# A graph kernel's pattern stage: three settle groups, gathered candidate rows and split degree sums

## The chip, the cores and the metric

The kernel runs on one core of one Trainium2 chip. The metric is device time in microseconds (us); lower is better. PE is TensorE, DVE VectorE, ACT ScalarE, POOL GpSimd and SP SyncE, whose queue here only issues DMAs. PSUM is the memory that PE writes its results to. Line numbers (L823) are those of the kernel before, unless a text says otherwise.

## What is computed

Four graph layers work on 16 graphs (batches) of 1024 nodes with 128 features. Only the second layer matters here. It takes the 0/1 pattern of the adjacency matrix and thins it by a rule that runs over the rows in order, because each row's removals also clear a column:

```python
def step(carry, n):
    row = jnp.take(carry, n, axis=0)
    nbi = row.astype(jnp.int32)
    num = jnp.sum(nbi)
    sf = jnp.where(num > T_DIL, (num + K_DIL - 1) // K_DIL, 1)   # T_DIL = 10, K_DIL = 2
    rank = jnp.cumsum(nbi)
    rm = row & (rank % sf == 0)
    valid = (mask_b[n] != 0) & (num > 1)
    rm = jnp.where(valid, rm, False)
    keep = ~rm
    carry = carry.at[n].set(row & keep)
    carry = carry.at[:, n].set(carry[:, n] & keep)
```

A node with at most ten neighbours left drops all of them (sf is 1); a node with more drops those at rank h and 2h, with h about half the count. The thinned matrix is then used in three graph convolutions. The kernel uses the fact that very little of the matrix survives: for each graph it finds the at most 128 "candidates" that still have more than ten neighbours when their turn comes, settles what they remove by a few rounds of a fixed-point iteration, and treats all other nodes as empty, apart from "lone" ones that keep their own diagonal entry. Flags would send the program to a general path; with these inputs they do not.

## The kernel before, in words

The program has four stages, one after the other: attention (to about 1700 us of the profile), the pattern stage (1700 to about 2095 us), three convolutions, and the end with layers 3 and 4. The attention stage has written the 0/1 mask of every graph to DRAM as `mask_d`, in fp16. The change touches only the pattern stage, `phase_pattern` from L656 on.

Three kinds of task make up that stage; each is a Python generator, and each `yield` ends a step.

- `find(b)`, L751, once for each of 16 graphs, 11 steps. It loads the graph's mask `m` (2 MB, L754, on the SP queue; the pool has three buffers for it). Degrees are column sums: 64 matmuls with a column of ones (L760), copied by ACT (L764). POOL makes the strictly upper diagonal blocks `md` (L767, eight multiplies). Three passes of `earlier` (L777 and L781, 36 matmuls each) count the neighbours that come before a node and drop out; after the third, the candidates are known. `slots` (L711) numbers them and makes a one-hot `oh` (L719). L804 and `nodes` (L728) turn this into rows and columns of node numbers; `keep.node` (L729, ACT) and `keep.index` (L731, DVE) hold them for gathers. L810 gathers the candidates' 128 rows of the adjacency matrix from DRAM, 512 KB, by an indirect DMA on POOL's queue. Eight ACT instructions make `le` (L817). L823 takes the candidates' columns out of the mask: 64 matmuls of 128 columns, `m` against `oh`. DVE masks that into `base` (L831); L837 (eight matmuls) gives ranks. At the end the gathered rows are turned (L854), copied (L856) and multiplied (L860) into `V`.
- `settle(g)`, L864, for eight graphs side by side, so its wide DVE operations have 8 x 128 elements per partition. It has five rounds: nine small DVE operations, three wide ones (L896 to L898), eight one-column matmuls (L901), a copy back (L903). Then follow rank tests, a transpose and the store to `slots_d`.
- `alone(b)`, L956, four steps for each graph once its settle is done: rank matmuls (L964), ACT and DVE tests (L970, L972), a second `slots` and two gathers. `inner` (L735) turns node numbers into indices for the gathers of `x1` rows (L746).

`rolling` (L635) sets the order. It keeps one list of at most five open tasks, in the order of the list, and opens the next only when the last opened one has made two steps and all that it needs has ended; in each turn each open task makes one step. The list is ten finds, settle 0, finds and alones in turn, settle 1, the other alones. A settle at the head of the list that isn't ready holds up all behind it. The framework then places instructions in each engine's queue, near this order, and each engine works its own queue in order. After the tasks come the last gathers of lone rows.

Of the kernel before, what the change touches and what calls it, by code (L numbers as in the profile page):

```python
# [22 lines left out]
B, N, F = 16, 1024, 128  # L23
# [590 lines left out]

KEEP = 10
ROUNDS = 5
HALF = B // 2


# [12 lines left out]
    arrays["q_one_up"] = np.ascontiguousarray(np.broadcast_to(node[:P], (P, P)))  # L632


def rolling(tasks, depth, lag):  # L635


    todo, active, ended = list(tasks), [], set()
    while todo or active:
        while (  # L640
            todo and len(active) < depth and (not active or active[-1][2] >= lag)
            and all(n in ended for n in todo[0][2])
        ):
            active.append([todo[0][0], todo[0][1], 0])
            todo.pop(0)
        for a in list(active):
            try:
                next(a[1])
                a[2] += 1
            except StopIteration:  # L650
                active.remove(a)
                ended.add(a[0])
# [3 lines left out]
def phase_pattern(ctx, tc, t, c, mask_d, slots_d, x1_d, keep, flags):  # L656
# [78 lines left out]
    def inner(k0, k1):  # L735

        k = slice(k0, k1)
        at = sm.tile([P, HALF], F32, name="at")
        none = sm.tile([P, HALF], F32, name="none")
        nc.vector.tensor_scalar(at, keep.node[:, k], -1.0, 0.0, op0=ALU.add, op1=ALU.max)  # L740
        nc.vector.tensor_scalar(none, keep.node[:, k], 0.0, float(N), op0=ALU.is_equal, op1=ALU.mult)
        nc.vector.tensor_copy(keep.inner[:, k], at)
        nc.vector.tensor_tensor(keep.row[:, k], at, none, ALU.add)
# [7 lines left out]
    def find(b):  # L751
# [2 lines left out]
        nc.sync.dma_start(m, mask_d[b].rearrange("(t p) n -> p t n", p=P))  # L754
        yield

        pu = ps_s.tile([P, T], F32, name="pu", tag="ps")
        for ni in range(T):
            for ci in range(T):
                nc.tensor.matmul(  # L760
                    pu[:, ni : ni + 1], m[:, ci, ni * P : (ni + 1) * P], one, start=ci == 0, stop=ci == T - 1
                )
        deg = sm.tile([P, T], F32, name="deg", bufs=6)
        nc.scalar.copy(deg, pu)  # L764
        md = wp.tile([P, T, P], F16, name="md", bufs=3)
        for ti in range(T):
            nc.gpsimd.tensor_tensor(md[:, ti, :], m[:, ti, ti * P : (ti + 1) * P], less, ALU.mult)  # L767
# [44 lines left out]
            bass.IndirectOffsetOnAxis(ap=keep.index[:, b : b + 1], axis=0),  # L812
        )

        le = wp.tile([P, T, P], F16, name="le", bufs=3)
        for ti in range(T):
            nc.scalar.activation(le[:, ti, :], row, AF.Sign, bias=half_up[:, ti : ti + 1])  # L817
# [1 line left out]

        pg = ps_b.tile([P, T, P], F32, name="pg", tag="pb")  # L820
        for ni in range(T):
            for ci in range(T):
                nc.tensor.matmul(  # L823
                    pg[:, ni, :], m[:, ci, ni * P : (ni + 1) * P], oh[:, ci, :],
                    start=ci == 0, stop=ci == T - 1,
                )
# [36 lines left out]

    def settle(g):  # L864

        bs = slice(g * HALF, (g + 1) * HALF)
        shape = [P, HALF, P]

        def tiny(name):
            return sm.tile([P, HALF], F32, name=name, bufs=3)  # L870

        def wide(name, dtype=F16):
            return lp.tile(shape, dtype, name=name)
# [6 lines left out]
        rb = RB[:, bs, :]  # L880
        for k in range(ROUNDS):
            num, h, big, top = tiny("num"), tiny("h"), tiny("big"), tiny("top")
            nc.vector.scalar_tensor_tensor(num, num0[:, bs], 1.0, gone, op0=ALU.add, op1=ALU.subtract)

            nc.vector.tensor_scalar(h, num, 0.5, 0.25, op0=ALU.mult, op1=ALU.add)
            nc.vector.tensor_scalar(h, h, ROUND, None, op0=ALU.add)
            nc.vector.tensor_scalar(h, h, ROUND, None, op0=ALU.subtract)
            nc.vector.tensor_scalar(big, num, float(KEEP), None, op0=ALU.is_gt)


            nc.vector.scalar_tensor_tensor(v1[:, bs], h, EDGE - 1, gone, op0=ALU.add, op1=ALU.add)
            nc.vector.tensor_tensor(top, v1[:, bs], h, ALU.add)
# [5 lines left out]
            nc.vector.tensor_tensor(rm, e1, e2, ALU.max)  # L898
            pn = ps_s.tile([P, HALF], F32, name="pn", tag="ps")
            for j in range(HALF):  # L900
                nc.tensor.matmul(pn[:, j : j + 1], rm[:, j, :], one, start=True, stop=True)  # L901
# [5 lines left out]
        inner(g * HALF, (g + 1) * HALF)  # L907
# [8 lines left out]
        for j in range(HALF):  # L916
# [15 lines left out]
        nc.vector.scalar_tensor_tensor(k1, num, 1.0, k1, op0=ALU.is_le, op1=ALU.max)  # L932
# [3 lines left out]
        for j in range(HALF):  # L936
# [13 lines left out]
        for j in range(HALF):  # L950
# [5 lines left out]
    def alone(b):  # L956

        pb = ps_b.tile([P, N], F32, name="prank", tag="pb")
        for ti in range(T):
            lo = ti * P  # L960
            for at in (0, N // 2):
                n0, n1 = max(lo, at), at + N // 2
                if n0 < n1:
                    nc.tensor.matmul(  # L964
                        pb[:, n0:n1], base[:, b, ti, :], run[:, n0 - lo : n1 - lo],
                        start=ti == 0, stop=n0 == lo and n1 == lo + P,
                    )
# [26 lines left out]
        yield  # L994

    tasks = [(f"f{b}", find(b), []) for b in range(HALF + 2)]
    tasks.append(("s0", settle(0), [f"f{b}" for b in range(HALF)]))
    for b in range(HALF - 2):
        tasks += [(f"f{HALF + 2 + b}", find(HALF + 2 + b), []), (f"a{b}", alone(b), ["s0"])]
    tasks.append(("s1", settle(1), [f"f{b}" for b in range(HALF, B)]))  # L1000
    tasks += [(f"a{b}", alone(b), ["s0"]) for b in (HALF - 2, HALF - 1)]
    tasks += [(f"a{b}", alone(b), ["s1"]) for b in range(HALF, B)]
    rolling(tasks, 5, 2)
    inner(B, B + HALF)
    inner(B + HALF, 2 * B)
    for k in range(B, 2 * B):
        rows_of_x1(k)


    nc.vector.tensor_scalar(keep.lone, keep.lone, 1.0, None, op0=ALU.min)  # L1010

# [1202 lines left out]
```

## Time and profile before

| | us |
|---|---|
| median of 10 runs | 3215.98 |
| lowest and highest run | 3210.03, 3223.99 |
| the profiled execution, its time | 3215.18 |
| the profiled execution, its span | 3213.2 |
| first matmul of the pattern stage (L760) | 1700.8 from the span's start |
| last matmul of the pattern stage (L728) | 2094.1 |

The profile is of one execution, taken by the hardware. It lists for each engine how long it was busy and what ended its idle time. Over the whole span PE is busy for 88%, DVE 70%, ACT 55% and POOL 40%; a busy share of PE overstates its work, since matmuls overlap and each is drawn with its full length. A view of one stretch gives the same per engine, with the clock that TensorE was granted (PEclk, 1.00 is full) and the share of time in which the 16 DMA engines worked. Between 1700 and 2095 us PE is busy for 290.8 us, DVE 232.2, ACT 104.2 and POOL 122.6, the mean granted clock is 0.73 and the DMA share 0.32.

### The profile page before, as it was taken

Reading aid. Unit: us, or ns where it says so; the run is one execution under the profiler, and the core shown is the slowest. Engines: PE = TensorE matmul, PEld = TensorE weight load, DVE = VectorE, ACT = ScalarE, POOL = GpSimd, SP = SyncE. Lnnn points to the kernel's source line nnn. Section 1 sums busy time; section 2 is a strip of 40 time slices with the busy share of each in tenths; the row PEclk is TensorE's granted clock in tenths of the full one; section 3 lists DMA queues with packets and bytes.
Section 4 is the critical chain, followed back from the end, with each engine's and each line's share of the span. In section 5 each row is a group of like instructions: output and inputs, shape, how many; then the busy total and the mean of one; then the engine's idle time right before and its main releaser. Section 6 shows DMA issues by size and latency. Waiting matters only on the chain. (4 is left out here: it accounts for less than half of the span.)

```text
span 3213.2 us, 70693 instructions
## 1 busy us (share of the span) xinstructions
PE 2812.8 (88%) x25724; PEld 2495.9 (78%) x25724; DVE 2250.2 (70%) x8226; ACT 1781.8 (55%) x5608; POOL 1271.5 (40%) x1280
## 2 busy tenths in 40 slices
PE   5999999999999999999997959467787899999997
PEld 3877877778777877778786858366676899999997
DVE  5887878788787878788784565745555566666665
ACT  3877777677776777677772323145644234333342
POOL 5544555454545454453113423243323323332221
PEclk9999999999999999999996767788988899999999
DMA  6422333223322332222023522043443434444441
GB/s 178 117 70 76 83 98 83 61 78 98 98 59 77 94 98 76 67 78 72 21 99 124 180 96 91 17 153 139 152 171 146 159 134 163 173 160 166 156 147 30
DMA packets 162024, 348.62 MB, mean 108 GB/s; under 512 B 14709, under 2 KB 68231, under 8 KB 161537
## 3 DMA queue, kind: packets, MB, share of 16 engines
q1 hardware_dynamic: 149760, 311.37, 30.7%
q0 software_dynamic: 10752, 28.42, 3.0%
q10 hardware_dynamic: 1152, 4.19, 0.4%
q8 instruction: 206, 3.38, 0.4%
q14 instruction: 154, 1.25, 0.1%
HBM read 257.87 MB, written 87.03 MB: 107 GB/s over the span
## 5 line engine op out<-in xcount | busy, mean ns | idle before, releaser
L272 POOL TENSOR_SCALAR mask<-ld 104x1024 f16<-104x1024 f32 (+1 forms) x150 | 441.4, 2942 | 555.3 <-PE pw L354 233.4
L434 PE MATMUL pg<-parts,oh 104*128 104x384 f32 (+1 forms) x1760 | 539.8, 383 | 49.6 <-ACT hg L452 48.9
L465 PE MATMUL pa<-hg,we 128*104 128x129 f32 (+1 forms) x3520 | 568.2, 277 | 1.9
L446 DVE SCALAR_TENSOR_TENSOR junk<-pg,w_a 128x128 f32<-128x128 f32 x1600 | 405.8, 284 | 177.4 <-PE pg L439 174.6
L465 PEld LDWEIGHTS pa<-hg,we 128*104 128x104 f32 x3520 | 497.7, 175 | 32.2 <-ACT hg L452 18.9
L452 ACT ACTIVATE hg<-pg,hg 128x128 f32<-128x128 f32 x1600 | 511.2, 371 | 17.1
L439 PE MATMUL pg<-parts,oh 104*128 104x384 f32 (+1 forms) x1760 | 473.4, 343 | 0.0
L434 PEld LDWEIGHTS pg<-parts,oh 104*128 104x128 f32 x1760 | 282.8, 193 | 78.5 <-ACT hg L452 61.8
L439 PEld LDWEIGHTS pg<-parts,oh 104*128 104x128 f32 x1760 | 315.3, 193 | 0.0
L450 ACT ACTIVATE hg<-sc 128x2 f32<-128x2 f32 (+1 forms) x880 | 188.5, 216 | 168.1 <-DVE junk L446 163.3
L419 DVE TENSOR_TENSOR we<-k_id,ids 128x832 f32<-128x832 f16 (+1 forms) x240 | 228.3, 951 | 8.4 <-PE pa L465 5.1
L1343 POOL TENSOR_TENSOR rstd<-ve,mhalf 128x4 f32<-128x4 f32 x96 | 97.0, 1010 | 324.4 <-DVE ve L1342 324.2
L389 ACT CAST oh<-oh_b 104x1024 fp32r<-104x1024 bf16 (+1 forms) x240 | 221.3, 978 | 2.1 <-DVE oh_b L385 2.0
L291 PE MATMUL pw<-w_all,xT 128*104 128x512 f32 x320 | 187.5, 670 | 17.2 <-DMA xT<-in_xTp 8.3
L1347 DVE TENSOR_SCALAR x<-x,mv,rstd 128x128 f32<-128x128 f32 x256 | 102.8, 443 | 91.1 <-POOL rstd L1343 91.1
L357 ACT CAST qs<-pw 104x416 f16<-104x416 f32 (+1 forms) x240 | 114.6, 478 | 66.9 <-PE pw L354 63.2
L385 DVE TENSOR_TENSOR oh_b<-pw,k_slot_edge 104x512 bf16<-104x512 f32 (+1 forms) x240 | 144.7, 635 | 9.7 <-PE pw L384 7.2
L364 DVE SCALAR_TENSOR_TENSOR one_way<-qs,mask 104x1040 bf16<-104x1040 f16 (+9 forms) x160 | 148.8, 930 | 0.1
L1452 ACT ACTIVATE y<-x,shift,rstd 128x128 f32<-128x128 f32 x128 | 52.7, 482 | 162.9 <-POOL shift L1445 162.9
L500 POOL TENSOR_TENSOR own<-parts 104x128 f32<-104x128 f32 x160 | 96.9, 641 | 115.5 <-DVE x_rows L521 79.5
L378 ACT CAST oh_b<-pw 104x512 bf16<-104x512 f32 (+1 forms) x240 | 133.2, 556 | 14.5 <-PE pw L377 14.4
L336 DVE TENSOR_TENSOR g<-k_slot,off 105x1408 f16<-105x1408 f16 x80 | 132.6, 1657 | 11.6 <-ACT off L332 11.5
(356 smaller groups left out, 6688.7 us busy)
## 6 DMA issues: line engine op xcount, KB each, us to landing
ld<-in_adjT SPq DMA_DIRECT2D x135, 416.0 KB
m<-mask_d SPq DMA_DIRECT2D x16, 2048.0 KB
keep_adj<-in_adjT SPq DMA_DIRECT2D x8, 4096.0 KB
adj<-in_adjT SPq DMA_DIRECT2D x8, 4096.0 KB
mask_d<-mask SPq DMA_DIRECT2D x144, 208.0 KB
hT_d<-uT SPq DMA_DIRECT2D x48, 512.0 KB
h<-hT_d SPq DMA_DIRECT2D x48, 512.0 KB
hT<-hT_d SPq DMA_DIRECT2D x32, 512.0 KB
```

Of the source, the lines that this page charges most:

```text
L272: engine.tensor_scalar(mt[:n, s, :N], ld[:n], 0.0, None, op0=ALU.is_gt)
L291: nc.tensor.matmul(pw[:W], xT[:, s * W : (s + 1) * W], w_all, start=True, stop=False, skip_group_check=True)
L364: nc.vector.scalar_tensor_tensor(junk[:W, :nb, :], q[:W, at : at + nb, :W], EDGE, mt[:W, i, i * W : NP].rearrange("p (n w) -> p n w", w=W) ...
L385: nc.vector.tensor_tensor(o[:W, n0 : n0 + m, 1, :], pw[:W, :m, :], k_slot_edge[:W].unsqueeze(1).to_broadcast([W, m, C]), ALU.is_equal,)
L389: nc.scalar.copy(wide.ends[:W, n0 : n0 + m], o[:W, n0 : n0 + m])
L419: nc.vector.tensor_tensor(we[:, :n, :], k_id.unsqueeze(1).to_broadcast([P, n, W]), wide.ids[:, 2 * lo : 2 * hi].unsqueeze(2).to_broadcast( ...
L434: nc.tensor.matmul(flat[:, first : 3 * F], own, d.parts[i][:W, p, first:], start=p == 0, stop=False, skip_group_check=True,)
L439: nc.tensor.matmul(pg[:, 1::step, :], other, reversed_parts(d.parts[j][:W, p, :], step), start=False, stop=p == 1, skip_group_check=True,)
L446: nc.vector.scalar_tensor_tensor(junk, pg[:, 1 + e, :], 0.0, w_a2, op0=ALU.max, op1=ALU.mult, accum_out=d.sc[:, at + e : at + e + 1],)
L450: nc.scalar.activation(hg[:, u - lo, :ways, F], d.sc[:, at : at + ways], AF.Exp)
L452: nc.scalar.activation(hg[:, u - lo, e, :F], pg[:, 3 - 3 * e, :], AF.Copy, scale=hg[:, u - lo, e, F : F + 1])
L465: nc.tensor.matmul(PA[bank][:W, at : at + part.stop - part.start], we[:, 2 * (u - lo) + e, :], hg[:, u - lo, e, part], start=False, stop=T ...
```

## The change

It has four parts, all in the pattern stage.

1. Groups. Settle runs for groups of 6, 6 and 4 graphs instead of 8 and 8. `rolling` has a limit for each kind of task: four finds, one settle, two alones (with which the gathers of lone rows of `x1` now count, one task for each group). A task that isn't ready no longer holds up those of another kind.
2. Candidates' rows gathered and turned. The 64 matmuls of L823 go. In their place a second indirect DMA gathers the candidates' 128 rows of the mask from DRAM (256 KB, the mask is symmetric), and eight matmuls with a diagonal matrix (`there`, one more DVE operation) turn them. `m` is not read any more after the third pass.
3. Degrees. The first four of eight 128-node blocks are row sums by ACT (a Relu over 1024 elements with an accumulator); the other four stay column sums on PE, 32 matmuls.
4. Small operations. A settle round has seven small DVE operations instead of nine, by keeping a rounding constant inside `h`.

```diff
+GROUPS = ((0, 6), (6, 12), (12, 16))
...
-def rolling(tasks, depth, lag):
+def rolling(tasks, most, lag):
...
+        for task in list(todo):
+            name, kind, steps, after = task
+            same = [a for a in active if a[1] == kind]
+            if len(same) < most[kind] and (not same or same[-1][3] >= lag) and ended.issuperset(after):
+                active.append([name, kind, steps, 0])
+                todo.remove(task)
...
+        deg = sm.tile([P, T], F32, name="deg", bufs=6)
+        for ti in range(T // 2):
+            junk = wp.tile([P, N], F16, name="hit1")
+            nc.scalar.activation(junk, m[:, ti, :], AF.Relu, accum_out=deg[:, ti : ti + 1])
         pu = ps_s.tile([P, T], F32, name="pu", tag="ps")
-        for ni in range(T):
+        for ni in range(T // 2, T):
...
-        deg = sm.tile([P, T], F32, name="deg", bufs=6)
-        nc.scalar.copy(deg, pu)
+        nc.scalar.copy(deg[:, T // 2 :], pu[:, T // 2 :])
...
+        marks = wp.tile([P, N], F16, name="marks")
+        nc.gpsimd.indirect_dma_start(
+            marks, None, mask_d.rearrange("b n m -> (b n) m"),
+            bass.IndirectOffsetOnAxis(ap=keep.index[:, b : b + 1], axis=0),
+        )
+
+        there = sm.tile([P, P], F16, name="there")
+        nc.vector.tensor_scalar(there, same, keep.node[:, b : b + 1], 1.0, op0=ALU.mult, op1=ALU.min)
...
         for ni in range(T):
-            for ci in range(T):
-                nc.tensor.matmul(
-                    pg[:, ni, :], m[:, ci, ni * P : (ni + 1) * P], oh[:, ci, :],
-                    start=ci == 0, stop=ci == T - 1,
-                )
+            nc.tensor.matmul(pg[:, ni, :], marks[:, ni * P : (ni + 1) * P], there, start=True, stop=True)
...
-            nc.vector.scalar_tensor_tensor(num, num0[:, bs], 1.0, gone, op0=ALU.add, op1=ALU.subtract)
-            nc.vector.tensor_scalar(h, num, 0.5, 0.25, op0=ALU.mult, op1=ALU.add)
-            nc.vector.tensor_scalar(h, h, ROUND, None, op0=ALU.add)
-            nc.vector.tensor_scalar(h, h, ROUND, None, op0=ALU.subtract)
+            nc.vector.scalar_tensor_tensor(num, num0[:, bs], 1.5, gone, op0=ALU.add, op1=ALU.subtract)
+            nc.vector.tensor_scalar(h, num, 0.5, ROUND, op0=ALU.mult, op1=ALU.add)
...
+    def lone_rows(g):
+        b0, b1 = GROUPS[g]
+        inner(B + b0, B + b1)
+        for k in range(B + b0, B + b1):
+            rows_of_x1(k)
+        yield
+
+    tasks = [(f"f{b}", "find", find(b), []) for b in range(B)]
+    for g, (b0, b1) in enumerate(GROUPS):
+        tasks.append((f"s{g}", "settle", settle(g), [f"f{b}" for b in range(b0, b1)]))
+        tasks += [(f"a{b}", "alone", alone(b), [f"s{g}"]) for b in range(b0, b1)]
+        tasks.append((f"x{g}", "alone", lone_rows(g), [f"a{b}" for b in range(b0, b1)]))
+    rolling(tasks, {"find": 4, "settle": 1, "alone": 2}, 2)
```

In the changed kernel's numbering the gather matmuls are L835, the indirect DMA of `marks` L821, the row sums L762 and `base` L840.

More of the change, by code (lines that the diff above doesn't have):

```diff
@@ L632, in pattern_constants @@
     arrays["q_one_up"] = np.ascontiguousarray(np.broadcast_to(node[:P], (P, P)))
-def rolling(tasks, depth, lag):
+def rolling(tasks, most, lag):
     todo, active, ended = list(tasks), [], set()
     while todo or active:
[L640 to L645, printed above, removed]
+        for task in list(todo):
[4 more added lines that the diff above has]
+                todo.remove(task)
         for a in list(active):
             try:
-                next(a[1])
-                a[2] += 1
+                next(a[2])
+                a[3] += 1
             except StopIteration:
@@ L737, in inner @@
         k = slice(k0, k1)
-        at = sm.tile([P, HALF], F32, name="at")
-        none = sm.tile([P, HALF], F32, name="none")
+        at = sm.tile([P, k1 - k0], F32, name="at")
+        none = sm.tile([P, k1 - k0], F32, name="none")
         nc.vector.tensor_scalar(at, keep.node[:, k], -1.0, 0.0, op0=ALU.add, op1=ALU.max)
@@ L864, in settle @@
     def settle(g):
-        bs = slice(g * HALF, (g + 1) * HALF)
-        shape = [P, HALF, P]
+        b0, b1 = GROUPS[g]
+        bs, n = slice(b0, b1), b1 - b0
+        shape = [P, n, P]
         def tiny(name):
-            return sm.tile([P, HALF], F32, name=name, bufs=3)
+            return sm.tile([P, n], F32, name=name, bufs=3)
         def wide(name, dtype=F16):
@@ L882, in settle @@
             num, h, big, top = tiny("num"), tiny("h"), tiny("big"), tiny("top")
-            nc.vector.scalar_tensor_tensor(num, num0[:, bs], 1.0, gone, op0=ALU.add, op1=ALU.subtract)
-            nc.vector.tensor_scalar(h, num, 0.5, 0.25, op0=ALU.mult, op1=ALU.add)
-            nc.vector.tensor_scalar(h, h, ROUND, None, op0=ALU.add)
-            nc.vector.tensor_scalar(h, h, ROUND, None, op0=ALU.subtract)
-            nc.vector.tensor_scalar(big, num, float(KEEP), None, op0=ALU.is_gt)
-            nc.vector.scalar_tensor_tensor(v1[:, bs], h, EDGE - 1, gone, op0=ALU.add, op1=ALU.add)
-            nc.vector.tensor_tensor(top, v1[:, bs], h, ALU.add)
+            nc.vector.scalar_tensor_tensor(num, num0[:, bs], 1.5, gone, op0=ALU.add, op1=ALU.subtract)
+            nc.vector.tensor_scalar(h, num, 0.5, ROUND, op0=ALU.mult, op1=ALU.add)
+            nc.vector.tensor_scalar(big, num, KEEP + 0.5, None, op0=ALU.is_gt)
+            nc.vector.scalar_tensor_tensor(v1[:, bs], h, EDGE - 1 - ROUND, gone, op0=ALU.add, op1=ALU.add)
+            nc.vector.scalar_tensor_tensor(top, h, -ROUND, v1[:, bs], op0=ALU.add, op1=ALU.add)
             nc.vector.scalar_tensor_tensor(top, top, -EDGE, big, op0=ALU.add, op1=ALU.mult)
@@ L898, in settle @@
             nc.vector.tensor_tensor(rm, e1, e2, ALU.max)
-            pn = ps_s.tile([P, HALF], F32, name="pn", tag="ps")
-            for j in range(HALF):
+            pn = ps_s.tile([P, n], F32, name="pn", tag="ps")
+            for j in range(n):
                 nc.tensor.matmul(pn[:, j : j + 1], rm[:, j, :], one, start=True, stop=True)
@@ L906, in settle @@
         nc.vector.tensor_scalar(below[:, bs], v2[:, bs], -0.5, None, op0=ALU.add)
-        inner(g * HALF, (g + 1) * HALF)
+        nc.vector.tensor_scalar(h, h, -ROUND, None, op0=ALU.add)
+        inner(b0, b1)
         up = wide("up")
@@ L915, in settle @@
         py = ps_b.tile(shape, F32, name="py", tag="pb")
-        for j in range(HALF):
+        for j in range(n):
             nc.tensor.matmul(py[:, j, :], up[:, j, :], run[:, :P], start=True, stop=True)
@@ L931, in settle @@
         nc.vector.tensor_tensor(k1, k1, big, ALU.mult)
-        nc.vector.scalar_tensor_tensor(k1, num, 1.0, k1, op0=ALU.is_le, op1=ALU.max)
+        nc.vector.scalar_tensor_tensor(k1, num, 1.5, k1, op0=ALU.is_le, op1=ALU.max)
         own = wide("own")
@@ L935, in settle @@
         pk = ps_b.tile(shape, F32, name="pk", tag="pb")
-        for j in range(HALF):
+        for j in range(n):
             nc.tensor.matmul(pk[:, j, :], same, low[:, j, :], start=True, stop=False)
@@ L949, in settle @@
         pt = ps_b.tile(shape, F32, name="pt", tag="pb")
-        for j in range(HALF):
+        for j in range(n):
             nc.tensor.transpose(pt[:, j, :], d[:, j, :], c.ident)
@@ L994, in alone @@
         yield
[L996 to L1007, printed above, removed]
+    def lone_rows(g):
+        b0, b1 = GROUPS[g]
+        inner(B + b0, B + b1)
[8 more added lines that the diff above has]
+    rolling(tasks, {"find": 4, "settle": 1, "alone": 2}, 2)
     nc.vector.tensor_scalar(keep.lone, keep.lone, 1.0, None, op0=ALU.min)
```

## The prediction

> **What bounds the kernel now.** I read the page's busy line first (span 3213.2 us; the profiled execution took 3215.18 us, 2.0 us more, and the median of the ten runs is 3215.98, so 0.8 us above the one I sum against). No engine is busy all through, so the share of PE (88%) says nothing about this stage. I then cut the pattern stage at events of the timeline: the first degree matmul (1700.8 us), the L837 matmuls of batch 0 (1737.0), batch 7 (1837.1) and batch 15 (2006.8), and the last L728 (2094.5), after which the next stage's loads go out.
>
> ```profile
> core 0: us, PE busy (x) PEld busy (x) DVE busy (x) ACT busy (x) POOL busy (x), PEclk, DMA share, GB/s
> 1700.80:1737.00 36.20, 27.74 (x701) 26.73 (x702) 11.38 (x37) 6.13 (x16) 13.77 (x33) 0.64 0.39 119
> 1737.00:1837.10 100.10, 91.98 (x1870) 90.71 (x1868) 48.47 (x121) 33.42 (x95) 38.02 (x64) 0.75 0.50 161
> 1837.10:2006.80 169.70, 128.85 (x2248) 119.21 (x2246) 105.41 (x265) 49.38 (x124) 49.52 (x71) 0.76 0.32 106
> 2006.80:2094.50 87.70, 42.26 (x414) 27.34 (x411) 66.43 (x181) 14.64 (x22) 20.62 (x21) 0.69 0.06 17
> ```
>
> Stretch A (100.1 us) is seven finds, 14.3 us each, with PE busy 92%. Stretch B (169.7) holds settle 0, eight finds and about six alones; nothing is full. Stretch C (87.7) is settle 1 and ten alones: DVE is 76% busy and PE waits for it. The groups of this stage give the prices:
>
> ```profile
> L823 PE MATMUL pg<-oh,m 128*128 128x128 f16 x1024 | 70.6, 238 | 0.8 <-DVE oh L719 0.8
> L767 POOL TENSOR_TENSOR md<-m,q_less 128x128 f16<-128x128 f16 x128 | 61.7, 516 | 54.0 <-DMA m<-mask_d 50.0 <-PE pu L781 3.7
> L760 PE MATMUL pu<-q_run,m 128*128 128x1 f16 x1024 | 29.1, 164 | 6.7 <-DMA m<-mask_d 4.5 <-ACT x1T L549 2.3
> L810 POOL DMA_INDIRECT rows<-in_adj,keep_index x16 | 21.7, 1359 | 81.0 <-issue 41.2 <-PE pu L781 34.2 <-DVE keep_index L731 5.7
> ```
>
> The columns are busy us, mean ns of one, and idle us before. L823 is the costliest thing on PE here (70.6/16 = 4.4 us a batch), and POOL waited 50 us for mask loads: a load needs a buffer that L823, the last reader, frees.
>
> **The change, part by part.** *Taken from PE*: L823 shrinks from 64 matmuls to 8. Eight 128-column fp16 matmuls are L804's shape, 0.61 us at 1752.7 and 1.06 at 1737.8, so 4.4 - 0.8 = 3.6 us a batch. Half of L760's 64 go: 29.1/16/2 = 0.9. Sum 4.5 us x 16 = 72 us of PE time. That would be the gain if PE alone set A; it does not once L823 is gone.
>
> *Added to ACT*: four Relu row sums a batch. The same form stands later in this kernel:
>
> ```profile
> L1462 ACT ACTIVATE neg<-adj x64: 1056/1057/1088, 2495.5 to 3147.5; 128x1024 bf16<-128x1024 f32 x64
> L1462 ACT ACTIVATION_READ_ACCUMULATOR neg<-adj x64: 185/187/221, 2496.4 to 3148.4; 128x1 f32 x64
> ```
>
> 4 x (1.06 + 0.19) = 5.0 us a batch, 80 us in all. ACT has 104 us of work in 393 us of stage, so about 185 after: it lies beside PE and DVE. Uncovered, each of the 16 sets costs 5.0 - 0.9 us on the way to the first pass. I take 2.5 us once, at the start, where nothing else runs (`keep_node` of batch 0 then stands behind three sets). Their output tile `hit1` is also that of the alones, so one can wait for an L972 (1.28 us); ACT has the room, 0.
>
> *Added to POOL and the DMAs, and put on the path*: `marks`, a second gather behind `rows`, and a wait for it. Before, gathered rows were needed three steps later (L854); now the next matmul of that batch needs them.
>
> ```profile
> keep_xs<-x_d,keep_inner POOLq DMA_INDIRECT x32, 3.3
> rows<-in_adj,keep_index POOLq DMA_INDIRECT x16, 4.9
> ```
>
> The last column is us from issue to landing: 3.3 for 64 KB, 4.9 for 512 KB. `marks` has 256 KB; bounds 3.3 and 4.9, I take 4.1, the middle. From the end of L728 to a landed `marks`: ACT copy and DVE index 0.4 (1753.48 to 1753.86), POOL start 0.8 (rows at 1754.63), `rows` 1.3, gap 0.3, then 4.1: 6.9 us.
>
> The Trainium skill, "DMA: Bandwidth & Descriptors", section "Anatomy of one DMA — SWDGE (gpsimd) path", fits such a transfer as 2.0 us plus bytes over 436 GB/s. By that, `rows` would take an estimated 3.2 us, where this trace has 4.9; the trace decides. With its 2.6 us for `marks`, every find below would be 1.5 us shorter, some 18 us over the twelve that wait longest.
>
> So the loop of a find is now a chain. In the changed program's PE order it runs gather matmuls of b, turn, L837 of b, node matmuls of b+1, some passes of others, gather matmuls of b+1. Behind the waiting gather stand, on PE, all of these and the passes of the other finds; on DVE `base`; on ACT the copies of both. Price: gather 0.7, `base` on DVE 1.2 + hops 0.6, L837 0.7, node matmuls 1.0, then 6.9: 11.1 us. What PE does meanwhile (passes 0.96 each, L860 2.0 to 3.8) is shorter and is hidden. On POOL, `md` of batch b+3 (3.1 us, 4.6 at worst) now stands ahead of `rows` and `marks` of b in most finds, and itself waits for a mask load (8.9 us from issue, 1726.3, to first use, 1735.2); I add 1.4 us as a mean, giving 12.5. At most four finds are open and they begin together, so every fourth one has to run its passes first: 22 us from gather to gather (pg, L837 2.5; two passes and turns on DVE 2.6; degrees, L860, third pass 5.5; slots, `oh`, nodes 4.5; 6.9). Mean (3 x 12.5 + 22)/4 = 14.9 us, against 14.3 now. **The gather takes the place of the 64 matmuls.** In A the seven finds lose 7 x 0.6 = 4.2. But batch 0 reaches L837 sooner: its nodes end at 1718.4, + 2.5 (ACT) + 6.9 + 0.7 + 1.8 = 1730.3 instead of 1737.0, since 64 matmuls (6.0 us at 1720.2) and a load stall (at 1735) are gone. A: 6.7 - 4.2, some 3 us gained.
>
> The Trainium skill speaks against the change at one more place: "TensorE: Matmul & The Clock Gate", Part 1, says that an idle window of about 3.4 us halves the array's clock. The rows agree that it moves here (L860 took 3.76 us at 1748.6 and 2.03 at 1759.7). The 22 us hold L860 at 3.5, so an array kept slow by the gather's waits is counted; with the fast L860 the mean would be 14.5 and A 3 us better.
>
> *Moved*: settles of 6, 6 and 4 batches beside finds and alones, each kind with its own limit. A settle round now costs 5.3 us alone (next fence).
>
> ```profile
> 2020.46 0.37 PE L901 MATMUL pn<-q_run,rm 128*128 128x1 f16 x8 [6.20 <-DVE rm L898]
> 2025.71 0.37 PE L901 MATMUL pn<-q_run,rm 128*128 128x1 f16 x8 [4.88 <-DVE rm L898]
> 2030.97 0.37 PE L901 MATMUL pn<-q_run,rm 128*128 128x1 f16 x8 [4.88 <-DVE rm L898]
> ```
>
> PE idles 4.9 of each 5.3 us, for DVE. In C that idle time is not covered, and in B, where settle 0 holds up the finds, hardly. The DVE work does not shrink: from its rows, 9 small ops of 0.18, two wide of 1.22, one of 0.70 and a copy 0.15 make 4.9; with 7 small ops and a width of 6 it is 3.8, of 4 it is 3.1. Five rounds and the rest (10.5 us of wide ops at width 8, plus 2.5) make 37, 29 and 23. An alone's rows sum to 3.5 (L972 1.28, L719 1.24, six small). C should then hold 37 + 35 = 72 and measured 66.4, since instructions overlap; times 0.92, settles are 34, 27, 21 and an alone 3.2. B's 105.4 then leaves 6.5 for a find; `there` adds at most 0.3 (L840's shape), I take 0.2.
>
> B after: eight finds 53.6, two settles 54, six alones 19.5: 127 us of DVE. The finds' chain would allow 8 x 14.9 = 119, so **DVE becomes the bound of B**. DVE was 76% full in C, the fullest stretch: 127/0.76 = 167; perfectly packed 127. With three kinds of work beside each other I take 0.80: 159, 11 us gained. C after: settle 2 and ten alones, 21 + 32 = 53 us of DVE; at the measured 0.76 it is 70, at 0.85 62; I take 65, 23 us gained. The last lone rows of x1 (L746, eight from 2096.4 on, 0.95 and a gap each) are halved, but they ran beside the next stage's loads (POOL idle 7.5 us before L1197 at 2113.6), so nothing. On SP a third store of `slots_d` is added, and that of settle 0 stands ahead of the last mask load, some 30 us before its use: nothing.
>
> Sum: 3 + 11 + 23 = 37 us. 3215.2 - 37 = **3178 us**. Bounds of the parts: A -15 to +15, B -10 to 45, C 10 to 35.
>
> **Rivals.** *1, the gather is hidden.* For it: PE, ACT and POOL have 9, 10 and 9 us a find, all below 14.9; the mask now goes free after the third pass, so loads run far ahead. Against it: only about 5 us of PE work stands between nodes and gather. Finds every 10.5 us give A 34; DVE at 0.90 in B gives 141, so 29; C 26. Sum 89: 3126.
>
> *2, DVE stands behind the gather: slower.* DVE works in order, and `base` (L840) waits for the gather; settle rounds and alones queue behind it, and POOL's `md` waits hold the gather back further. If DVE stands w us a find in B, B is 150 + 8w. It is slower once 8w exceeds 20 + 26, so from w = 5.7. At 10 us (6.9, plus `md` and its load in part) B is 230, a loss of 60 against 26 gained: 3249. For it: the order on DVE really has `base` ahead of settle ops. Against it: those ops can stand before it too, and PE's own waits are shorter than 6.9.
>
> *3, no change*: w near 5, 3209 to 3222.
>
> **How the numbers follow.** A measurement here tells 0.2% (6.4 us) from nothing. My forecast (3140 to 3209) has 0.56, rival 1 0.22, rival 3 0.07, rival 2 0.15. Faster 0.78, same 0.07, slower 0.15. The range takes in rival 1 and stops short of rival 2: 3112 to 3220.
>
> **What would show it.** Right: gather matmuls (L835) with idle time released by DMA `marks`, several us on most of 16; finds still 13 to 16 us apart up to batch 7; `m` waits of POOL and ACT nearly gone; DVE near 80% from batch 8 on; the tail after batch 15 about 65 us. Wrong: L835 not waiting (rival 1), or DVE idle before L840 with pn matmuls over 10 us apart (rival 2). An ACT on the path would show as `keep_node` behind L762, which I have priced at almost nothing.

## The result and the profile after

The changed kernel took 3226.28 us in the median of 10 runs (3218.74 to 3231.24), against 3215.56 for the kernel before beside it: a ratio of 1.0032, 95% interval 1.0018 to 1.0045. It is slower by 0.3%, where 1.2% faster was forecast. The profiled execution took 3224.02 us, its span is 3222.2, 9.0 more than before. Of these 9.0, the pattern stage has 6.6; the rest lies in stages that the change doesn't touch (attention ended 3.5 us sooner, all after the pattern stage took 5.9 us longer). In a second profile of the same kernel the stages behind it took 1.9 us less than in the first.

The changed kernel's stage, cut at the same events (first degree matmul L766, L846 of batches 0, 7 and 15, last L730); columns as before:

```profile
core 0: us, PE busy (x) PEld busy (x) DVE busy (x) ACT busy (x) POOL busy (x), PEclk, DMA share, GB/s
1697.30:1734.40 37.10, 16.23 (x453) 15.55 (x454) 15.68 (x38) 20.89 (x47) 18.55 (x41) 0.50 0.48 159
1734.40:1852.90 118.50, 74.89 (x1142) 71.29 (x1141) 53.53 (x126) 64.25 (x153) 48.41 (x73) 0.62 0.46 157
1852.90:2021.80 168.90, 110.44 (x1830) 97.15 (x1830) 112.89 (x339) 67.75 (x163) 53.06 (x67) 0.68 0.33 106
2021.80:2097.60 75.80, 42.60 (x394) 27.39 (x394) 56.90 (x187) 15.29 (x24) 26.69 (x26) 0.73 0.09 23
```

Stretch A, the seven finds alone, grew by 18.4 us (100.1 to 118.5) although PE has 17 us less to do in it. B is the same (169.7 to 168.9), C is 11.9 us shorter (87.7 to 75.8). What PE lost in work came back as idle time. The group of the gather matmuls in the changed kernel, busy and mean ns, then the idle time before it:

```profile
L835 PE MATMUL pg<-there,marks 128*128 128x128 f16 x128 | 15.0, 286 | 71.9 <-DMA marks<-mask_d,keep_index 71.9
```

15.0 of work and 71.9 of wait stand where 70.6 of work and 0.8 of wait stood (L823). The waits of the stage, in us, times, longest:

```profile
PEld L835 <- DMA marks<-mask_d,keep_index: 77.7, 15, 10.1
PE pg L835 <- DMA marks<-mask_d,keep_index: 71.9, 15, 10.1
DVE base L840 <- PE pg L835: 69.1, 14, 9.3
POOL md L772 <- DMA m<-mask_d: 65.9, 9, 25.5
POOL rows L815 <- DVE there L827: 41.5, 8, 11.2
```

Both in-order engines of the find stand: PE for the landing, and DVE at `base` for PE. In the kernel before, DVE's idle time ahead of `base` was small, 17.9 us in all (last column), where it is now 70.6:

```profile
L831 DVE TENSOR_TENSOR base<-pg,stay 128x1024 f16<-128x1024 f32 x16 | 19.5, 1221 | 17.9 <-PE pu L715 10.4 <-PE pg L823 7.5
```

One find of the changed kernel's timeline (start, duration, engine; idle time in brackets) shows the chain from node numbers to the gather matmuls:

```profile
1736.09 0.40 PE L730 MATMUL pc<-q_node,oh 128*128 128x1 f16 x8
1736.53 0.16 ACT L731 COPY keep_node<-pc 128x1 f32<-128x1 f32 x1 [0.90 <-PE pc L730]
...
1738.33 0.16 DVE L795 SCALAR_TENSOR_TENSOR s<-deg,pu 128x8 f16<-128x8 f32 x1 [0.73 <-PE pu L717]
1738.48 0.14 DVE L733 TENSOR_SCALAR keep_index<-keep_node 128x1 int32<-128x1 f32 x1
...
1738.90 1.88 POOL L815 DMA_INDIRECT rows<-in_adj,keep_index  x1 [3.55 <-DVE there L827]
...
1741.08 0.95 POOL L821 DMA_INDIRECT marks<-mask_d,keep_index  x1 [0.30 <-issue]
...
1748.57 1.04 PE L835 MATMUL pg<-there,marks 128*128 128x128 f16 x8 [5.67 <-DMA marks<-mask_d,keep_index]
1748.91 1.20 POOL L772 TENSOR_TENSOR md<-m,q_less 128x128 f16<-128x128 f16 x3 [5.05 <-DMA m<-mask_d]
1749.64 1.23 DVE L840 TENSOR_TENSOR base<-pg,stay 128x1024 f16<-128x1024 f32 x1 [6.05 <-PE pg L835]
```

The index is made 1.8 us after the ACT copy, since it stands behind the use of a pass's result on DVE; `rows` takes 1.88 us to issue, and `marks` needs 7.5 us from issue to use. POOL's next `md` waits for a 2 MB mask load that was issued at 1737.5, and its data arrive in the same half microsecond as `marks`. The trace's packet records show more: from 1738 to 1744 the mask load's packets move and none of the gathers' (the view of 1742 to 1744 has 392 GB/s); those of the gathers, issued at 1738.9 and 1741.1, first move at 1744, and from then on both kinds move side by side until 1748.5. Two finds later no load is running: the gathers' packets start 2.6 us after the issue of `rows`, not 5.1, and `marks` lands in 4.0 us. Since `m` goes free after the third pass, a load is now often issued just ahead of the gathers, 0.1 to 3.0 us before `rows` in eight of the 16 finds. From issue to landing, `marks` took 4.0 to 10.1 us (median 5.1).

### The profile page after: what moved, and what is told of

Read it like the earlier page. It is cut to its first block, busy times and chain, and to the rows that moved or that the text cites. A ratio compares the mean times of both kernels' runs of the same rounds, so it can differ in the third digit from the quotient of the medians.

```text
span 3222.2 us, 68125 instructions
## 1 busy us (share of the span) xinstructions
PE 2768.2 (86%) x24316; PEld 2445.8 (76%) x24316; DVE 2260.8 (70%) x8312; ACT 1845.9 (57%) x5737; POOL 1288.2 (40%) x1296
## 5 line engine op out<-in xcount | busy, mean ns | idle before, releaser
L336 DVE TENSOR_TENSOR g<-k_slot,off 105x1408 f16<-105x1408 f16 x80 | 132.6, 1658 | 11.9 <-ACT off L332 11.8
```

## The experiments

**Theory 1**: PE, and DVE behind it, wait in each find for the gathered mask rows; the wait has taken the place of the removed matmuls. **Theory 2**: the limit of four open finds makes bursts of four with a hole of 28 to 36 us behind each. **Theory 3**: the row sums on ACT delay the passes. The table has each kernel's ratio to the kernel before on the same chip, and, from one profile each, the stage's stretches (to batch 0's pr, A, B, C; C ends here at the start of the last L730 group, some 0.4 us sooner than in the views).

| kernel | ratio, 95% interval | to pr 0 | A | B | C |
|---|---|---|---|---|---|
| before | 1 | 36.1 | 100.1 | 169.7 | 87.3 |
| changed | 1.0032 (1.0018 to 1.0045) | 37.0 | 118.5 | 169.0 | 75.4 |
| changed, again | 1.0040 (1.0025 to 1.0055) | 36.7 | 119.8 | 170.2 | 74.9 |
| no gather | 0.9912 (0.9894 to 0.9931) | 37.9 | 101.9 | 153.2 | 71.8 |
| no gather, again | 0.9924 (0.9903 to 0.9944) | 38.3 | 93.3 | 163.6 | 83.3 |
| gather alone | 1.0115 (1.0093 to 1.0136) | 33.2 | 119.4 | 184.4 | 86.6 |
| all degrees on PE | 1.0028 (1.0014 to 1.0042) | 33.5 | 120.4 | 169.9 | 75.2 |
| mask held | 1.0039 (1.0022 to 1.0056) | 39.8 | 118.1 | 176.5 | 75.6 |
| groups alone | 0.9956 (0.9940 to 0.9972) | 36.0 | 98.1 | 169.2 | 82.8 |
| gather unread | 0.9958 (0.9943 to 0.9974) | 37.9 | 99.1 | 162.3 | 83.0 |
| gather unread, again | 0.9937 (0.9917 to 0.9956) | 38.1 | 97.9 | 166.2 | 83.0 |
| five finds | 1.0008 (0.9993 to 1.0022) | 37.0 | 120.4 | 158.9 | 84.4 |
| no gather, five finds | 0.9915 (0.9896 to 0.9935) | 38.1 | 96.9 | 144.6 | 93.4 |
| read a step later, five finds | 0.9938 (0.9920 to 0.9956) | 38.6 | 105.7 | 145.2 | 92.6 |
| both, alternating | 1.0189 (1.0169 to 1.0210) | 42.4 | 140.8 | 196.9 | 68.7 |
| both, 64 first | 1.0035 (1.0019 to 1.0052) | 37.9 | 110.8 | 178.5 | 82.3 |

Single profiles of the same kernel agree within 2 us for the changed one, but within 14 for the one without the gather: in its second run (beside which the kernel before took 3223 us, not 3214), DVE and ACT show waits of 2 to 9 us, 28 in sum and most of them after A, whose releaser the profile doesn't show. Every profile taken where the kernel before was at 3223 to 3225 us has such waits (8 to 51 us in sum; the groups alone, the two with the gather unread, the one with a constant in the gather's place, the three with five finds, the kernel with all 64 first), and no other profile has any. So the ratios decide, and stretches only between profiles without such waits or where the difference is large.

### Without the gather

```diff
-        marks = ... ; nc.gpsimd.indirect_dma_start(marks, ...) ; there = ...
+            for ci in range(T):
+                nc.tensor.matmul(pg[:, ni, :], m[:, ci, ni * P : (ni + 1) * P], oh[:, ci, :], ...)
-            nc.tensor.matmul(pg[:, ni, :], marks[:, ni * P : (ni + 1) * P], there, start=True, stop=True)
```

> The changed kernel with the gather of the candidates' mask rows taken back: the 64 matmuls against the loaded mask block make pg again; the three groups, the new task order and the row sums on ACT stay. Theory 1 (TensorE and then VectorE wait each find for the gathered mask rows): the stretch from the first find's pr to the eighth's falls from 118.5 us to 100 to 104, the last one stays near 76, and the kernel is at 3200 to 3208 us, 18 to 26 under the changed kernel. Theory 2 (the limit of four open finds makes bursts of four with a hole behind each): the stretch stays at 112 to 119, the kernel at 3216 to 3226. Theory 3 (the row sums on ACT delay the passes): the same 3216 to 3226, with ACT's work just ahead of the degrees' end.

0.9912, with 3186.96 us in the median: better than theory 1 said. A is back at 101.9. Its first two stretches, for the clock:

```profile
1702.80:1740.70 37.90, 24.46 (x572) 23.93 (x573) 12.51 (x37) 19.25 (x41) 12.54 (x30) 0.62 0.33 104
1740.70:1842.60 101.90, 83.08 (x1467) 80.39 (x1464) 48.81 (x119) 60.94 (x151) 41.42 (x68) 0.78 0.51 167
```

PE does 8 us more in A (83.08 against 74.89) and ends 16.6 us sooner. The holes between bursts are still there (1771.1 to 1803.1, 1842.6 to 1878.6), so they aren't the gather's. Stretch by stretch, the changed kernel with the gather takes 0.9 us less to batch 0's pr, 16.6 more in A, 15.8 more in B and 3.6 more in C (neither of the two profiles has unexplained waits).

> The same kernel as the one without the gather before (ratio 0.991), beside the next three on one chip, since the chip of the second four runs showed the kernel before at 3225 us and not at 3214. If the gain is the kernel's and not the chip's, the ratio is again 0.989 to 0.994; if the row sums on ACT and the lack of traffic were flattered by the first chip, it is 0.995 to 0.997.

0.9924: the gain is the kernel's.

### The gather alone, put into the kernel before

> The kernel before with only the gather of the candidates' mask rows and its 8 matmuls in place of the 64; two groups, five tasks at once and 64 degree matmuls stay as they were. Two small buffers are single ones to make room. Theory 1: the gather costs by itself what the change lost in its first two stretches, and the last stretch's 11.9 us aren't gained: 3228 to 3240 us. Theories 2 and 3 (the gather costs nothing, the limit or the row sums do): 3205 to 3218 us.

1.0115, 3251.21 us: 1.2% slower, 11 us above the range of theory 1, far from that of the others. Its waits:

```profile
PEld L830 <- DMA marks<-mask_d,keep_index: 84.1, 16, 7.7
PE pg L830 <- DMA marks<-mask_d,keep_index: 81.2, 16, 7.3
DVE base L835 <- PE pg L830: 73.3, 15, 7.7
```

(Three buffers, of `marks`, `there` and a scratch tile, are single ones in this kernel; what that adds isn't shown.) With and without the rest of the change, the gather costs 1.1 to 1.2%, some 35 to 39 us. It is the loss; it ate the 0.8% or so that the other parts gain.

### All degrees on PE, and the groups alone

```diff
-        for ti in range(T // 2):
-            nc.scalar.activation(junk, m[:, ti, :], AF.Relu, accum_out=deg[:, ti : ti + 1])
-        for ni in range(T // 2, T):
+        for ni in range(T):
```

> The changed kernel with all degrees as column sums on TensorE again (64 matmuls in place of 32, no row sums on ACT); gather and groups stay. Theory 3 (row sums on the path): 3208 to 3216 us. Theory 1 and theory 2: within 5 us of the changed kernel's 3226, since the added 32 matmuls stand where TensorE waits for the gather in any case; a little slower if they stand ahead of the first pass of a burst.

1.0028: nothing changed, and theory 3 falls. Only the way to batch 0's pr is 3.5 us shorter (33.5, not 37.0), where nothing covers ACT. PE's work for degrees goes from 16.2 to 29.2 us and vanishes in the wait.

> The changed kernel with the gather of mask rows and the row sums on ACT both taken back: of the change only the three groups, the new task order and the shortened scalar steps stay. The kernel without the gather alone taken back stood at 3187 us (0.991 of the kernel before). If the row sums only cost (3.5 us until batch 0's pr, as the two kernels with the gather show), this one is at 3180 to 3186 us. If they help once TensorE no longer waits for the gather (32 degree matmuls a find less on TensorE's path), it is at 3190 to 3210 us. If the groups gained nothing, it would be at 3205 or above.

0.9956: the groups, the task order and the shorter scalar steps gain 0.44%, some 14 us. Beside 0.9912 and 0.9924 without the gather, the row sums may gain 0.3 to 0.4% as soon as PE doesn't wait, but that isn't shown: they were timed on different chips, and the interval overlaps that of one of the two runs without the gather, and not the other's.

### Is it the landing, or the work of the gather?

> The changed kernel with the gather still issued for every batch, but pg made by the 64 matmuls from the loaded mask block, so that nothing waits for the gathered mask rows. If the loss is the wait for the landing (theory 1), it is near the kernel without the gather: 3185 to 3200 us. If the loss comes from the gather's own traffic or from GpSimd, which issues it ahead of the next diagonal blocks and adjacency rows, it stays at 3212 to 3230 us.

0.9958, 3211.57 us: between my two ranges, and 0.46% above the first run without the gather, which was on another chip. On one chip, beside the kernel without the gather:

> The same kernel as the one whose gather is issued and not read (ratio 0.996), beside the kernel without the gather on one chip. If the traffic and the issue on GpSimd cost by themselves, it stays 0.3 to 0.6% above the kernel without the gather; if only the wait costs, the two agree within 0.2%.

0.9937 beside 0.9924: inside the intervals, the DMAs and POOL's issue cost little or nothing (0.1%, at most 0.4%). The changed kernel, which does wait for the rows, is 0.7 to 1.0% above the two runs with the gather unread: the wait is the larger part of the loss.

> The changed kernel with the gathered mask rows given time to land: the mask rows are gathered ahead of the adjacency rows, the 8 matmuls that read them stand one step of the task order later, and five finds may be open in place of four so that others fill the step. If waiting for the landing is the whole loss (theory 1), TensorE's waits for the mask rows fall from 72 us to under 25 and the kernel is at 3180 to 3205 us. If what the wait held up was late anyway (the three mask buffers, VectorE), it stays at 3215 to 3230 us though the waits go.

```diff
-        rows = ... ; marks = ...
+        marks = ... ; rows = ...
...
         yield
+        yield
         pg = ps_b.tile([P, T, P], F32, name="pg", tag="pb")
...
-    rolling(tasks, {"find": 4, "settle": 1, "alone": 2}, 2)
+    rolling(tasks, {"find": 5, "settle": 1, "alone": 2}, 2)
```

0.9938. Who waits for `marks` in it (us, times):

```profile
who waited for it (us, times):
  PEld L836: 40.5, 13
  PE pg L836: 35.0, 12
  DVE base L841: 19.7, 9
```

PE's wait has halved, not fallen under the 25 us that I expected, and most of DVE's is gone; the kernel is 0.6% ahead of before. Five finds, the order of the two gathers and the later read came together here. It is still no better than the one without the gather: 64 matmuls fewer a find bought nothing that the time shows.

> The changed kernel as it is, with five finds open at once in place of four. Theory 2: the holes between bursts (28 to 36 us) shrink and the kernel is at 3195 to 3212 us, ahead of the kernel before. Theory 1 alone: each find still waits for its landing, 3215 to 3228 us.

1.0008: five finds alone give back 0.24% (the intervals just touch), and A stays at 120. Theory 2 explains a small part at most.

> The kernel without the gather, with five finds open at once in place of four. Theory 2 (the limit of four makes the holes of 32 to 36 us between bursts): 10 to 25 us faster than with four, 0.983 to 0.988 of the kernel before. If the three mask buffers and VectorE make the holes, within 6 us of the kernel with four.

0.9915, the same as with four. It is level with the best here: both versions without the gather beat both kernels of the case.

### How much is the landing itself, how much the collision with the load?

```diff
         nc.vector.tensor_tensor(base[:, b], pg, stay, ALU.mult)
+        held = sm.tile([P, 1], F32, name="held", bufs=2)
+        nc.vector.tensor_tensor(held, pg[:, 0, :1], m[:, T - 1, N - 1 :], ALU.mult)
```

> The changed kernel with one tiny VectorE operation added that reads the mask block and pg, so the block's buffer is let go only when the gather's matmuls have ended, and the next 2 MB mask load can't run beside the gather. Theory 1 with the collision as its cause: the mask rows land in 4 to 5 us in nearly every find (in the changed kernel 7 to 10 in half of them), and TensorE's waits for them fall from 72 us to under 45; what the later load costs then shows at the next find's first operations, so the time lies between 3212 and 3226 us. Theory 1 without the collision (the landing is late because of its own queue): landings stay at 4 to 10 us, the waits at 65 to 75, and the time is 3228 to 3240 us.

1.0039. With the mask held, as the tile's view gives it:

```profile
  PEld L835: 57.8, 15
  PE pg L835: 54.9, 15
...
DMA to landing us min/median/max: 4.2/4.8/8.3
```

The landings are shorter and the wait falls by 17 us, but not under the 45 I expected: 55 us remain. The time doesn't move; the loads now come late (POOL waits 103.8 us for `m`, not 65.9), which probably takes back what the gathers gained.

> The changed kernel with the mask load cut to an eighth: only the first 128 rows of each mask block are loaded (256 KB in place of 2 MB) and stand for all eight chunks, so the groups found are not the reference's, and only this stage's stretches are read, not the whole time. No long load can run beside a gather. If the collision with the mask load is what made the gather cost, the mask rows land in 4 to 5 us each time and this stage is within 15 us of the same kernel without the gather. If a bare landing of 4 to 5 us a find already costs, the stage stays 20 to 35 us above it.

> The kernel without the gather with the same cut load (an eighth of each mask block stands for all of it, so the groups are not the reference's, and only the stage is read). It is what the one with the gather and short loads is compared with: its stage is expected at 335 to 365 us, under the 365 to 379 us with whole loads by what the waits for the loads were worth.

```diff
-        m = mp.tile([P, T, N], F16, name="m")
-        nc.sync.dma_start(m, mask_d[b].rearrange("(t p) n -> p t n", p=P))
+        m1 = mp.tile([P, N], F16, name="m")
+        nc.sync.dma_start(m1, mask_d[b, :P])
+        m = m1.unsqueeze(1).to_broadcast([P, T, N])
```

Wrong groups send the program down its general path (21 ms), so only the stage counts. With the gather, the tile's view and stretch A:

```profile
DMA to landing us min/median/max: 3.9/4.3/4.8
```

```profile
1730.70:1832.50 101.80, 70.88 (x1143) 67.25 (x1141) 51.73 (x125) 63.51 (x153) 48.06 (x68) 0.68 0.25 75
```

And A without it:

```profile
1734.10:1823.90 89.80, 80.88 (x1533) 79.33 (x1530) 50.97 (x121) 60.86 (x150) 42.66 (x68) 0.85 0.23 68
```

The stages are 366.7 and 341.6 us, 25.1 apart; with whole loads they are 399.9 and 364.8 (changed, and no gather), 35.1 apart. None of the four profiles has unexplained waits. So by them some two thirds of the loss is the bare landing of 4.3 us in the chain, and the collision is the smaller part. This is an estimate: one profile each, and in the second pair with other data.

> The changed kernel with a constant tile of ones in place of the gathered mask rows, and no gather of them: the 8 matmuls read the constant, so the groups that this kernel finds are not those of the reference. It is what the change would be if the gather were free and instant. If TensorE's 64 matmuls a find are on the path once nothing waits for a landing (the rival of the prediction in which the gather is hidden, 3126 us), it is at 3125 to 3160 us. If VectorE, the mask loads and the limit of four set the pace by then, it is near the kernel without the gather, 3170 to 3190 us, and the change had little to win even with a free gather.

The whole time can't be read here either, for the same reason. Stretch A:

```profile
1734.50:1838.60 104.10, 70.11 (x1142) 67.57 (x1140) 54.89 (x126) 59.70 (x145) 43.51 (x69) 0.64 0.48 161
```

The stage took 373.6 us with a free gather, against 365 to 379 without the gather (the 379 and this one have unexplained waits, all of this one's behind A). With neither the 64 matmuls nor a wait for `marks`, A is no shorter than with the matmuls (101.9, and 93.3 in the second profile). So the second case holds, as far as one profile tells: there was next to nothing to win. Late next is the other gather: PE's transposes then wait 38.0 us for `rows`.

### Is it the cold clock?

A's granted clock is 0.62 in the changed kernel and 0.78 without the gather. To fill the wait, both kinds of matmuls were done.

> The changed kernel with both: TensorE first does the 64 matmuls from the mask block again (4.4 us a find in the kernel before), into the same place, then the 8 gather matmuls overwrite it. If the removed matmuls lay on TensorE's path in the changed kernel, it is 30 to 60 us slower than the changed kernel. If they fit wholly into the wait for the mask rows, and the wait's cold clock (0.62 in the first seven finds, 0.78 without the gather) costs nothing, it is within 5 us of it. If the cold clock is part of the loss, the granted clock comes back to 0.7 or more and it is 5 to 20 us faster than the changed kernel, though it does more work.

1.0189. This one told something else than I wanted. Written block by block, the kinds alternate on PE, and 56 of the 64 ran behind the first gather matmul. From that one to the end the finds take 3.7 to 5.9 us, where the eight gather matmuls by themselves take 0.6 to 1.0 (in the next kernel); the whole cost is 50 us (1.0189 less the 1.0035 of the next kernel), 3.1 us a find. So most of what was added behind the landing shows in the time.

> As the kernel with both kinds of matmuls (1.019), but all 64 from the mask block stand ahead of the 8 gather matmuls on TensorE; there, the two kinds alternated block by block, so that 56 of the 64 ran only after the mask rows had landed. Now they can run inside the wait. If the wait had 4 us of room a find and the cold clock costs nothing, 1.002 to 1.006 of the kernel before, like the changed kernel. If the cold clock is part of the loss, 0.997 to 1.001. If the matmuls delay the next find's chain even so, 1.008 or more.

1.0035 with all 64 ahead, the time of the changed kernel, though PE has its 64 matmuls back in every find. Its stretch A:

```profile
1741.20:1852.00 110.80, 86.93 (x1524) 84.25 (x1522) 48.97 (x126) 61.19 (x150) 45.11 (x75) 0.79 0.56 184
```

The clock is back at 0.79, and PE waits 27.9 us for `marks` in the whole stage, not 71.9. The removed work fits into the wait. A is 8 us shorter and B 9 us longer (this profile has the unexplained waits), and the warmer clock pays nothing that the whole time shows. This kernel also holds `m` longer; holding the mask alone moved nothing (1.0039).

> The changed kernel as it is, beside the kernel with both kinds of matmuls on one chip: 1.002 to 1.005 of the kernel before, with its stage at 395 to 405 us in a second profile. A stage outside of that would say that differences of under 10 us between single profiles mean little.

1.0040, the stage at 401.6 us (399.9 in the first profile).

## Why the prediction was wrong

The step that failed is "**the gather takes the place of the 64 matmuls**", priced at 14.9 us a find against 14.3: the way from node numbers to gather matmul was put at 6.9 us and took 10.8, most of it in the landing of `marks` (4.1 put, 6.7 measured), and the removed matmuls, taken as an equal exchange, weren't what a find lasts.

| step | predicted | measured |
|---|---|---|
| end of nodes to gather matmul | 6.9 | 10.8 (mean of batches 1 to 7, from the starts in the timeline) |
| of it: ACT copy and DVE index | 0.4 | 1.6 |
| of it: POOL's start | 0.8 | 0.3 |
| of it: issue of `rows`, and the gap | 1.6 | 2.2 |
| of it: `marks` from issue to use | 4.1 | 6.7 |
| one find to the next in a burst | 12.5 | 15.1 (six in A) |
| at a burst's end | 22 | 28.6 |
| batch 0's L837 | 6.7 sooner | 0.9 later |
| A, B, C (gain) | 3 with the start, 11, 23 | -19.3 with the start, 0.8, 11.9 |

**The landing was mis-sized.** The 4.1 us came from two gathers of the kernel before, and it holds where no load was issued just ahead: in batches 3 and 7 of the changed kernel `marks` lands in 4.0 us, and the whole way is 6.9 us, as forecast. I had noted that `m` goes free sooner and counted it as a help (loads run far ahead); it is also what puts a load beside the gather. With the collision gone (short loads), the landing is 4.3 us and the finds come (1790.9 - 1728.2)/4 = 15.7 us apart, near my 14.9. So the chain was drawn rightly in the main; besides the landing, the copy and the index took 1.2 us more than I had, with the index in its turn on DVE.

**The comparison was wrong too.** I set 14.9 against 14.3. But without the gather the rest of the change brings the finds to (1842.6 - 1740.7)/7 = 14.6 us, or 13.3 in the second profile, and the same kernel with short loads to 12.8; and with neither the matmuls nor the wait (the free gather) they come 104.0/7 = 14.9 us apart. The 64 matmuls are not what a find lasts. By the short loads this is the larger error: with a landing of 4.3 us, near the forecast one, the gather still costs 25.1 us of the stage, where I had put 0.6 us a find. "72 us of PE time ... would be the gain if PE alone set A; it does not" was right, and I then still took the cover as a free exchange.

**The two rules.** The shortest landing of `marks` here was 3.9 us, the longest 10.9; the fit in the Trainium skill, "DMA: Bandwidth & Descriptors", section "Anatomy of one DMA — SWDGE (gpsimd) path", which gives an estimated 2.6, is further off than my 4.1.

The granted clock was 0.62 in A and 0.78 without the gather, and the rule on idle windows in "TensorE: Matmul & The Clock Gate", Part 1, of the Trainium skill goes with that; filling the wait brought the clock back and no time with it.

**B.** I said that DVE becomes the bound, with 127 us of work at 0.80. It had 112.9 us of work at 0.67 (112.9/168.9), so it wasn't full. The other parts did gain there what I forecast and more: without the gather B takes 153.2 us, 16.5 less than before (163.6 in the second profile, with unexplained waits). With the gather B takes 15.8 more, and that is nearly the whole gain; DVE stood 27.7 us at `base` here.

**C.** Right in kind, half in size: 56.9 us of DVE work at a density of 0.75, where I had 53 at 0.82. The groups alone are worth about 14 us in the whole time, and I had hoped for 34 in B and C.

**The start.** Row sums: 3.5 us, I had 2.5. The first `marks` took 8.3 us to land, beside the mask load, and not 4.1.

**The rivals.** Rival 2's mechanism, DVE standing at `base` behind the gather, is what happened (69.1 us), but not in its place: per find it is 3.5 us in B (27.7/8), under its threshold of 5.7, and 5.3 in A (36.9/7), where I had assumed that nothing on DVE would care. Its B of 230 us never came. Rival 1 (hidden, 3126) is refuted: the gather isn't hidden, and even a constant in its place saves 20 us of the stage, not 89 (one profile). My sign that would prove the forecast right, finds 13 to 16 us apart, is missed with a mean of 18.3 (73.1 us for the first four gathers). Three other signs are missed too: POOL's waits for `m` were to be nearly gone and rose from 50.0 to 65.9 us, DVE was to be near 80% from batch 8 on and is at 67% in B, and the tail after batch 15 was to be 65 us and is 75.8.

## What to carry to other kernels

Before work is traded for a DMA, ask whether the removed work lay on the path, and whether the new wait does: here 70.6 us of matmuls filled time that a chain needed anyway, and 71.9 us of wait took their place, in which an in-order engine could not reach what stood behind it. A landing is priced beside what will be in flight at that moment in the changed kernel, above all a transfer that the change itself sets free earlier. And parts that came together are timed apart: without its gather this change is 0.8% faster than before.

## What the runs showed of the hardware

A 256 KB gather, issued behind a 512 KB one, landed in 3.9 to 4.8 us with no 2 MB load running and in up to 10.9 us beside a 2 MB load of another queue. In the changed kernel's trace the gathers' first packets moved 4.2 to 5.5 us after the issue of `rows` where a load had been issued 0.1 to 3.0 us before it (eight finds), and 1.6 to 2.6 us after it where none was running (seven finds). In the kernel before, beside loads issued 5.0 to 7.0 us ahead, it was 2.0 to 2.6 us (four finds). Once they moved, both queues' packets shared the time. What holds the gather back at its start, no run here says.

The issue of the `rows` gather on POOL took 1.60 us in the mean (1.36 before). A second gather behind it isn't the reason by itself: with one, it took 1.37 to 1.39 us in the gather alone, all degrees on PE and the gather unread. The waits without a releaser are up to 10.7 us each, in kernels with and without the gather; their cause stays open.
